# The pair loop of a graph network in the source's order on four engines, with two graphs prepared side by side

## The chip, the cores and the metric

The kernel runs on one core of a Trainium2 chip. The core's engines have queues of their own: PE (TensorE: matrix products into PSUM), DVE (VectorE: elementwise work), ACT (ScalarE: activations and copies), POOL (GpSimd: here indirect transfers and small copies) and SP (SyncE: here only the issue of DMA transfers). Each works through its instructions in the order of its queue. The metric is the time on the device in microseconds, the median of several runs.

## What is computed

The input is 16 graphs of 1024 nodes with 64 channels each, a dense 0/1 adjacency matrix of 1024 x 1024 for each graph, and a mask. Layer 0, cut to what matters:

```python
h = relu(layernorm(x))
neigh = (adj > 0) & ~eye
rank  = cumsum(neigh) - neigh                  # number of a neighbour in its row
nb    = neigh.sum(-1)
skip  = where(nb > 10, (nb + 1) // 2, 1)
rem   = neigh & (skip > 1) & (rank % skip == skip - 1) & mask
rem   = rem | rem.T
living = where(rem, 0, adj or eye) > 0
s  = sort(h of the living neighbours)          # for every node and channel
nv = living.sum()
for tau, w in ((0.25, 0.25), (0.5, 0.5), (0.75, 0.25)):
    agg += w * (s interpolated at tau * (nv - 1))
x = x + mask * (relu((h + agg) @ W1 + b1) @ W2 + b2)
```

Layer 1 is a layernorm, three graph convolutions with `adj` (each a product, a bias, a relu and a scaling), their concatenation through one more product, a relu, and the sum with `x`.

## The kernel before

Two graphs make a pair: with 64 channels each they fill the 128 partitions. There are eight pairs. For a pair the kernel first *prepares*, then *gathers* and *sorts* blocks of nodes.

**Preparing** (`prepare`, L585, with `prepare_one` for each graph of the pair, L654). Layernorm of `x` (L560 to L568) and a store of `h`. For each of eight tiles of 128 rows: a load of `adj` into tile `a` (L664, 512 KB, two buffers), its sign as `edge` on ACT (L671), a test of the values on DVE (`junk_v`, L673), eight transposes on PE (`ptE`, L678), and a copy from PSUM to `edgeT` on ACT (L681). Then a store of `edgeT` to memory (`adjT_d`, L684), sums of chunks of 128 columns, numbers of neighbours and skips (`own` L686, `nbp` L691, L695 to L706), the rank test (`cs` on PE, L716 and L721; `stays` on ACT, L725; the comparison on DVE, L726), the removal (`q` on PE, `edge` on ACT, L752), a key by which nodes are put in order of their number of neighbours (`key` L758, `keys` L763 on PE, eight passes `junk` on ACT, L770, `place` on DVE, L773), and eight indirect scatters on POOL that write the rows of the living edges by place (`live_d`, L778). Then `find_live` fetches these rows (`lp`, L794, on POOL's queue), transposes them (`pt`, L809; `liveT`, L812), and counts (`sums`, `nv_all`, `by`), and `number_slots` gives each living neighbour its slot number (`pr` on PE, L845 and L847; `r` on ACT, L851). `z` (L615 to L618) and `hp`, `h` in three parts of 16 bits (L625 to L628), come at the end.

**Gathering** (`gather`, L959). Nodes lie in order of their number of neighbours, in seven blocks (0 to 200, 392, 592, 768, 888, 960 and 1008, with 11 to 26 slots) and a tail of 16 nodes with 42 slots. For a group of slots DVE compares the slot numbers with constants (one-hot tile `s`, L987, two buffers), PE multiplies it with `hp` into `pg` (L1018, three buffers in PSUM, 48 products of up to 400 columns for a full group), and ACT copies `pg` to `g` (L1023).

**Sorting** (`quantiles`, L925, in `sort_block`). A sorting network on DVE: elementwise minima and maxima between two arrays `g` and `t` (L935). Weights of the quantiles come from two ACT passes for each slot (`coef`, L868 and L871); DVE multiplies and adds (L941, L950) into `agg`.

**The order.** `weave` (L1106) runs through the sort of block n operation by operation and calls other generators' steps by the share of the sort that is done: the gather of block n + 1 over the window −0.2 to 0.9, and the preparation of the next pair (`ahead`) in `SHARES[n]` steps of a total of 93:

```python
SHARES = (10, 9, 17, 24, 20, 13, 0)
```

Preparation goes graph after graph, copies from PSUM stand directly behind the products that they empty, and the last block of a pair runs beside block 0 of the next (L1457). This is the source's order. The queue of each engine is set by a scheduler of the framework, which takes the source's order as a priority and reorders by its own costs. A hint (`after=` in `send` and `store`, L1032 to L1053) holds back the transposes of finished aggregates. The pair loop is at L1438. Before it lies the prologue (constants, `prepare(0)`, the gather of block 0), after it the late stage (last pair, tails, MLP, layer 1).

Of the kernel before, what the change touches and what calls it, by code (L numbers as in the profile page):

```python
# [10 lines left out]
F32 = mybir.dt.float32  # L11
# [11 lines left out]
P = 128  # L23
C = 64
# [6 lines left out]
SHARES = (10, 9, 17, 24, 20, 13, 0)  # L31
# [348 lines left out]
class Steps:  # L380


    def __init__(self, gen):
        self.gen, self.result = gen, None

    def step(self):
        if self.gen is None:
            return False
        try:
            next(self.gen)  # L390
        except StopIteration as e:
            self.gen, self.result = None, e.value
            return False
        return True

    def rest(self):
        while self.step():
            pass


@with_exitstack
def graph_layers_kernel(ctx: ExitStack, tc: tile.TileContext, ins, out: bass.AP):
# [182 lines left out]
    def prepare(p, pools):  # L585
# [6 lines left out]
        xt, h, sq = room[:, 0], room[:, 1], room[:, 2].rearrange("p x t c -> p (x t) c")  # L592
        for x in range(2):
            nc.sync.dma_start(out=xt[:, x], in_=rows_of(x_d[2 * p + x]))
        flat = "p x t c -> p (x t) c"
        layernorm_relu(work, h.rearrange(flat), xt.rearrange(flat), sq, T2)
        for x in range(2):
            nc.sync.dma_start(out=rows_of(h_d[2 * p + x][:, :]), in_=h[:, x])
        yield
# [5 lines left out]
        find_live, number_slots = [], []  # L605
        for x in range(2):
            find_live.append((yield from prepare_one(st, x, pools)))
        for x in range(2):
            number_slots.append((yield from find_live[x]()))
            yield from number_slots[x](0)  # L610


        st.z = keep.tile([P, len(TAUS), N], BF16, tag="z", name="z")
        half = work.tile([P, N], F32, tag="a", bufs=2, name="half")
        nc.vector.tensor_scalar(half, st.nvs, 0.498, MAGIC, ALU.mult, ALU.add)  # L615
        nc.vector.tensor_scalar(half, half, MAGIC, None, ALU.subtract)
        for q, (tau, _) in enumerate(TAUS):
            nc.vector.scalar_tensor_tensor(st.z[:, q, :], st.nvs, -tau, half, ALU.mult, ALU.add)  # L618
# [5 lines left out]
        st.hp = keep.tile([P, 3, 2, NT, C], BF16, tag="hp", bufs=2, name="hp")  # L624
        nc.scalar.copy(st.hp[:, 0], h)  # L625
        nc.vector.tensor_tensor(h, h, st.hp[:, 0], ALU.subtract)
        nc.scalar.copy(st.hp[:, 1], h)
        nc.vector.tensor_tensor(st.hp[:, 2], h, st.hp[:, 1], ALU.subtract)  # L628
        yield
        st.number = itertools.chain(*(number_slots[x](1) for x in range(2)))  # L630
# [7 lines left out]
    def chunk_sums(eT, pools):  # L638

# [11 lines left out]
        nc.scalar.copy(sums, tot)  # L651
        return sums

    def prepare_one(st, x, pools):  # L654
        work, keep, ps = pools
# [5 lines left out]
        edgeT = work.tile([P, NT, N], F8, tag="byte", bufs=4, name="edgeT")  # L661
        def load(t):
            a = work.tile([P, N], F32, tag="a", bufs=2, name="a")
            nc.sync.dma_start(out=a, in_=adj_d[b, t * P : (t + 1) * P, :])  # L664
            return a

        coming = load(0)
        yield
        for t in range(NT):
            a, coming = coming, load(t + 1) if t + 1 < NT else None  # L670
            nc.scalar.activation(edge[:, t, :], a, AF.Sign, saturate=False)  # L671
            junk = work.tile([P, N], F8, tag="junk_v", name="junk_v")
            nc.vector.scalar_tensor_tensor(  # L673
                junk, a, 1.0, a, ALU.is_equal, ALU.not_equal, accum_out=odd[:, b, t : t + 1], saturate=False
            )
            pt = ps.tile([P, NT, P], F32, tag="big", bufs=2, name="ptE")
            for u in range(NT):
                nc.tensor.matmul(  # L678
                    out=pt[:, u, :], lhsT=edge[:, t, u * P : (u + 1) * P], rhs=ident_h, start=True, stop=True
                )  # L680
            nc.scalar.activation(edgeT[:, :, t * P : (t + 1) * P], pt, AF.Copy, saturate=False)  # L681
            yield

        nc.sync.dma_start(out=adjT_d[b][:, :, :], in_=edgeT)  # L684
        own = diagonal(edgeT)
        nc.vector.tensor_tensor(own, own, other_h[:, None, :].to_broadcast([P, NT, P]), ALU.mult, saturate=False)  # L686
        yield
        sums = chunk_sums(edgeT, pools)
# [5 lines left out]
        nb = work.tile([P, NT], F32, tag="nb", name="nb")  # L694
        nc.vector.tensor_copy(nb, nbp)  # L695


        act = work.tile([P, NT], F32, tag="act", name="act")
        nc.vector.scalar_tensor_tensor(act, nb, MIN_DEG, mk, ALU.is_gt, ALU.mult)
        skip = work.tile([P, NT], F32, tag="skip", name="skip")  # L700
        nc.vector.tensor_scalar(skip, nb, 0.5, 0.25, ALU.mult, ALU.add)
        nc.vector.tensor_scalar(skip, skip, MAGIC, MAGIC, ALU.add, ALU.subtract)
        back = work.tile([P, NT], F32, tag="back", name="back")
        nc.vector.tensor_scalar(back, skip, -3.0, 1.0, ALU.mult, ALU.add)
        look = work.tile([P, NT], F32, tag="look", name="look")
        nc.vector.scalar_tensor_tensor(look, skip, 1.0, act, ALU.add, ALU.mult)  # L706
        nc.vector.tensor_scalar(look, look, 1.0, None, ALU.subtract)
        yield
# [3 lines left out]
        for t in range(NT):  # L712
# [12 lines left out]
            nc.scalar.activation(stays[:, t, :], cs, AF.Abs, bias=back[:, t : t + 1], scale=2.0)  # L725
            nc.vector.tensor_scalar(stays[:, t, :], stays[:, t, :], look[:, t : t + 1], None, ALU.not_equal)  # L726
            if t % 2:
                yield

        nv = work.tile([P, NT], F32, tag="nv", name="nv")  # L730
        for t in range(NT):
            q = ps.tile([P, N], F32, tag="big", bufs=2, name="q")
            for hf in range(NH):
# [18 lines left out]
            nc.scalar.activation(  # L752
                edge[:, t, :], q, AF.Relu, bias=bias(-2.0), accum_out=nv[:, t : t + 1], saturate=False
            )
            yield

        key = work.tile([P, NT], F32, tag="key", name="key")
        nc.vector.scalar_tensor_tensor(key, nv, float(N), node, ALU.mult, ALU.add)  # L758
        minus = work.tile([P, NT], F32, tag="minus", name="minus")
        nc.vector.tensor_scalar(minus, key, -1.0, None, ALU.mult)  # L760
        keys = ps.tile([P, N], F32, tag="big", bufs=2, name="keys")
# [5 lines left out]
        above = work.tile([P, NT], F32, tag="above", name="above")  # L767
        for t in range(NT):
            junk = work.tile([P, N], F8, tag="junk", name="junk")
            nc.scalar.activation(  # L770
                junk, keys, AF.Sign, bias=minus[:, t : t + 1], accum_out=above[:, t : t + 1], saturate=False
            )
# [14 lines left out]
        yield  # L787
        def find_live():


            liveT = work.tile([P, NT, N], F8, tag="byte", bufs=4, name="liveT")
            def fetch(t):
                lp = work.tile([P, N // 4], I32, tag="lp", bufs=2, name="lp")
                load = nc.gpsimd.dma_start(out=lp, in_=live_d[b][t * P : (t + 1) * P, :])  # L794
# [6 lines left out]
                return lp.bitcast(F8)  # L801

            coming = fetch(0)
            yield
            for t in range(NT):
# [32 lines left out]
            def number_slots(side):  # L838

                j0, j1 = ((0, SPLIT), (SPLIT, N))[side]  # L840
                for u in range(NT):
# [10 lines left out]
                    if u % 2:  # L852
                        yield

            return number_slots

        return find_live

# [679 lines left out]
```

## Time and profile before

| what | value |
|---|---|
| runs | 3157.66, 3168.78, 3170.39 us (median 3168.78) |
| profiled execution | 3163.56 us, span 3161.8 us |
| granted clock of PE over the span | 0.915 |
| POOL's largest group: `live_d` scatters (L778) | 128, 261.1 us |
| copies of `pg` on ACT (L1023) | 384, 169.0 us busy, 399.4 us of idle time before them |

The page gives the busy time of each engine, the chain of work that ended last, and groups of instructions by line. In a group's row "<-" stands between what is written and what is read; "x" is the count; then follow the busy time and the mean in nanoseconds of one; then the engine's idle time just before instructions of this group, and what ended most of it. Idle time of an engine that isn't the bottleneck costs nothing by itself. The chain of waits gives shares of the span. In tables by window the first figures are the window and its length, then busy time of PE, PEld (weight loads), DVE, ACT and POOL with counts, then the granted clock of PE, the DMA engines' share and GB/s. Rows of waits give engine, tile and line, the releaser, the sum in us, the number of times, and the longest.

### The profile page before, as it was taken

The page shows a single profiled execution, that of the slowest core. Times are in us where ns is not written, and L with a number is a line of the kernel's source. Part 1 is how long each engine was busy: PE and PEld are TensorE (multiplying, and loading weights), DVE is VectorE, ACT ScalarE, POOL GpSimd, SP SyncE. Part 2 cuts the span into 40 slices and gives each one's busy share as a digit, 9 for nine tenths or more (in the row PEclk, how much of TensorE's full clock was granted, in tenths as well). Part 3 has the DMA queues.
Part 4 walks back from the last instruction along what each step waited for, and adds up shares of the span by engine and source line. Part 5 has one row for each costly group of instructions (what it writes and reads, how often), then busy time and mean ns, then how long its engine had stood idle before and what let it go on. Part 6 is the DMA issues. An engine that isn't in the chain of part 4 may idle for free.

```text
span 3161.8 us, 67201 instructions
## 1 busy us (share of the span) xinstructions
PE 2599.2 (82%) x27849; PEld 1697.4 (54%) x27849; DVE 2559.8 (81%) x5895; ACT 1696.2 (54%) x3292; POOL 619.5 (20%) x545
## 2 busy tenths in 40 slices
PE   2678978898888889885798889888986688977778
PEld 1445655565556556653565566456643456644445
DVE  4149889998999799989998999899976979963332
ACT  4764666567557755774367557745853223332221
POOL 5110161022102200330022103300422530311110
PEclk9779999999899999997899999999987799988989
DMA  4131022111211212122111211211113011122211
GB/s 138 46 104 60 3 67 70 56 55 52 66 57 54 64 56 68 46 72 47 42 64 51 66 56 57 67 56 63 48 36 75 9 41 26 49 55 54 54 54 42
DMA packets 221082, 177.45 MB, mean 56 GB/s; under 512 B 189024, under 2 KB 189152, under 8 KB 216672
## 3 DMA queue, kind: packets, MB, share of 16 engines
q1 hardware_dynamic: 141824, 125.88, 13.1%
q0 software_dynamic: 17408, 37.81, 3.9%
q10 hardware_dynamic: 61536, 9.39, 1.7%
q8 instruction: 219, 3.59, 0.5%
q14 instruction: 95, 0.78, 0.1%
HBM read 124.44 MB, written 48.55 MB: 55 GB/s over the span
## 4 chain that ended last, share of the span: by engine, by line
DVE 40%; PE 29%; ACT 12%; DMA 8%; issue 6%; another core or an unknown queue 2%; POOL 2%; ACTq 1%; DVEq 0%; POOLq 0%; SPq 0%
PE pg L1018 11%; DVE t L935 10%; DVE s L987 9%; DVE g L935 8%; PE pg L1200 5%; ACT junk L770 3%; DMA a<-in_adj 3%; DMA lp<-live_d 3%; DVE junk_v L673 2%; PE pr L845 2%; DVE g_tails L935 1%; DVE t_tails L935 1%; PE keys L763 1%; PE pf L1216 1%
## 5 line engine op out<-in xcount | busy, mean ns | idle before, releaser
L1018 PE MATMUL pg<-s,hp 128*64 128x400 bf16 (+11 forms) x16848 | 1366.5, 313 | 172.3 <-DVE s L987 138.1
L1018 PEld LDWEIGHTS <-hp 128*64 128x64 bf16 x16848 | 894.5, 112 | 553.9 <-issue 109.6
L987 DVE TENSOR_SCALAR s<-r 128x3200 bf16<-128x3200 bf16 (+25 forms) x1312 | 623.6, 521 | 103.6 <-PE pg L1018 74.9
L778 POOL DMA_INDIRECT live_d<-edge,place x128 | 261.1, 2040 | 1354.3 <-DVE place L773 1149.9
L1023 ACT COPY g<-pg 128x400 f32<-128x400 f32 (+10 forms) x384 | 169.0, 443 | 399.4 <-PE pg L1018 363.1
L935 DVE TENSOR_TENSOR t<-g 128x600 f32<-128x600 f32 (+9 forms) x524 | 315.5, 626 | 34.0 <-ACT g L1023 33.2
L1200 PE MATMUL pg<-adjT,xw 128*64 128x512 fp8e4 x2304 | 284.5, 398 | 52.8 <-ACT xw L1185 25.7
L935 DVE TENSOR_TENSOR g<-t 128x96 f32<-128x96 f32 (+16 forms) x555 | 283.2, 537 | 1.2
L1243 POOL DMA_INDIRECT agg<-agg_d,place x128 | 171.2, 1338 | 495.2 <-PE pt L1131 258.2
L671 ACT ACTIVATE edge<-a 128x1024 fp8e4<-128x1024 f32 x128 | 135.1, 1058 | 214.4 <-DMA a<-in_adj 213.9
L1200 PEld LDWEIGHTS <-xw 128*64 128x64 bf16 x2304 | 140.1, 114 | 182.4 <-issue 42.0
L868 ACT ACTIVATE coef<-z,bias 128x200 f32<-128x200 bf16 (+6 forms) x480 | 173.9, 405 | 102.3 <-DVE agg L950 66.0
L935 DVE TENSOR_TENSOR t<-t 128x192 f32<-128x192 f32 (+20 forms) x447 | 207.8, 475 | 0.2
L871 ACT ACTIVATE coef<-coef,wcol 128x200 f32<-128x200 f32 (+7 forms) x512 | 189.6, 403 | 9.3 <-issue 7.1
L673 DVE SCALAR_TENSOR_TENSOR junk_v<-a 128x1024 fp8e4<-128x1024 f32 x128 | 155.4, 1214 | 24.4 <-DMA a<-in_adj 24.4
L845 PE MATMUL pr<-liveT,upto 128*128 128x512 fp8e4 (+2 forms) x384 | 127.4, 350 | 53.1 <-ACT r L851 46.9
L770 ACT ACTIVATE junk<-keys,minus 128x1024 fp8e4<-128x1024 f32 x128 | 144.3, 1128 | 38.1 <-PE keys L763 34.3
L851 ACT CAST r<-pr 128x592 bf16<-128x592 f32 (+1 forms) x256 | 142.5, 585 | 41.1 <-PE pr L847 32.1
L794 POOL DMA_DIRECT2D lp<-live_d x128 | 89.4, 699 | 376.9 <-PE pt L809 319.3
L812 ACT ACTIVATE liveT<-pt 128x1024 fp8e4<-128x1024 f32 x128 | 130.3, 1034 | 50.5 <-PE pt L809 47.1
L752 ACT ACTIVATE edge<-q,bias 128x1024 fp8e4<-128x1024 f32 x128 | 141.8, 1108 | 22.6 <-PE q L747 22.6
L725 ACT ACTIVATE stays<-cs,back 128x1024 f16<-128x1024 f32 x128 | 136.7, 1111 | 31.1 <-PE cs L721 15.9
(182 smaller groups left out, 3879.4 us busy)
## 6 DMA issues: line engine op xcount, KB each, us to landing
a<-in_adj SPq DMA_DIRECT2D x128, 512.0 KB
adjT_d<-edgeT SPq DMA_DIRECT2D x16, 1024.0 KB
lp<-live_d POOLq DMA_DIRECT2D x128, 128.0 KB
adjT<-adjT_d SPq DMA_DIRECT2D x16, 1024.0 KB
room<-in_x SPq DMA_DIRECT2D x16, 256.0 KB
h_d<-room SPq DMA_DIRECT2D x16, 256.0 KB
h_again<-h_d SPq DMA_DIRECT2D x16, 256.0 KB
xt<-in_x SPq DMA_DIRECT2D x16, 256.0 KB
```

The lines of the kernel that those rows point to most:

```text
L673: nc.vector.scalar_tensor_tensor(junk, a, 1.0, a, ALU.is_equal, ALU.not_equal, accum_out=odd[:, b, t : t + 1], saturate=False)
L770: nc.scalar.activation(junk, keys, AF.Sign, bias=minus[:, t : t + 1], accum_out=above[:, t : t + 1], saturate=False)
L778: sent = nc.gpsimd.indirect_dma_start(out=live_d[b][:, :], out_offset=bass.IndirectOffsetOnAxis(ap=place[:, b, t : t + 1], axis=0), in_=ed ...
L845: nc.tensor.matmul(out=pr[:, o], lhsT=upto, rhs=liveT[:, u, sl], start=True, stop=(u == 0))
L868: nc.scalar.activation(coef[:, i, :], z[:, at], AF.Abs, bias=bias(rank - (slots + 1) // 2 + tau), scale=sign)
L871: nc.scalar.activation(coef[:, i, :], coef[:, i, :], AF.Relu, bias=wcol[:, q : q + 1], scale=-w)
L935: nc.vector.tensor_tensor(view(bufs, o, n1, n2), view(bufs, a, n1, n2), view(bufs, b, n1, n2), ALU.max if op else ALU.min)
L987: nc.vector.tensor_scalar(s[:, k, :, us, w0:], r[:, :, us, at + w0 : at + W], float(LIVE + 1 + k0 + k), None, ALU.is_equal)
L1018: summed = nc.tensor.matmul(out=pg[x * C : (x + 1) * C, ks, w0:], lhsT=st.hp[:, part, x, u, :], rhs=s[:, ks, x, u, w0:], start=(whole and ...
L1023: nc.scalar.copy(g[:, k0 : k0 + n, :], pg)
L1200: nc.tensor.matmul(out=pg[cs, :], lhsT=part[:, u, cs], rhs=adjT[x][:, u, sl], start=(u == 0 and k == 0), stop=(u == NT - 1 and k == len(xw ...
L1243: nc.gpsimd.indirect_dma_start(out=agg[:, t, x, :], out_offset=None, in_=agg_d[b][:, :], in_offset=bass.IndirectOffsetOnAxis(ap=place[:, b ...
```

## The change

The loop over pairs stands in a region in which DVE, PE, ACT and SP take their instructions in the source's order; POOL, the prologue and the late stage stay with the scheduler. The source's order is written anew:

- A step may hand back a callable (mostly the copy of a PSUM tile on ACT). `Steps` runs it at the start of the next step, so that it stands one step later in the queues. A callable may hand back another (the comparison after `stays`, the next two of the eight passes over `keys`).
- The two graphs of a pair are prepared in turns (`in_turns`), the second 22 turns behind the first. `find_live` and the first half of the numbering are part of `prepare_one`. The second half of the numbering of pair p opens the preparation of pair p + 1. Shares are new, 171 steps in all.
- Two tiles `a` are loaded ahead where one was, and two tiles `lp`. The fetch of `lp` goes from POOL's queue to SP's.
- A gather is a pipeline: step i copies group i − 2, makes the one-hot tile of group i, and multiplies group i − 1. Its window is 0 to 0.92; the tail's gather stands ahead of block 6's and ends at 0.4. The hint in `send` is gone.
- The activations of `coef` are spread over the first 0.6 of the sort.
- `z` is made by `make_z` after the last block of a pair, with the copies to `tail_z` on POOL.

The diff, cut to its core:

```diff
-SHARES = (10, 9, 17, 24, 20, 13, 0)
+SHARES = (25, 23, 30, 40, 30, 23, 0)
+
+BEHIND = 22
...
     def step(self):
+        self.left = [more for more in [f() for f in self.left] if more]
         if self.gen is None:
-            return False
+            return bool(self.left)
         try:
-            next(self.gen)
+            more = next(self.gen)
         except StopIteration as e:
             self.gen, self.result = None, e.value
-            return False
+            return bool(self.left)
+        if callable(more):
+            self.left.append(more)
         return True
...
+def in_turns(one, other, ahead=0):
+
+    results = [None, None]
+    left = [one, other]
+    while any(left):
+        for k in range(2):
+            if k and ahead > 0 and left[0]:
+                continue
+            if left[k]:
+                try:
+                    more = next(left[k])
+                except StopIteration as e:
+                    left[k], results[k] = None, e.value
+                    continue
+                yield more
+            if not k:
+                ahead -= 1
+    return results
...
-    def prepare(p, pools):
+    def prepare(p, pools, before=None):
...
+        if before is not None:
+            yield from before
...
+        sums = yield from in_turns(*(prepare_one(st, x, pools) for x in range(2)), BEHIND)
         yield
 
         h = work.tile([P, 2, NT, C], F32, tag="a", bufs=2, name="h_again")
         for x in range(2):
             nc.sync.dma_start(out=h[:, x], in_=rows_of(h_d[2 * p + x][:, :]))
...
+        yield
+        yield
+        nc.scalar.copy(hp[:, 0], h)
+        yield
+        nc.vector.tensor_tensor(h, h, hp[:, 0], ALU.subtract)
...
+        def edges(t):
+            if t < NT:
+                a = coming.pop(t)
+                nc.scalar.activation(edge[:, t, :], a, AF.Sign, saturate=False)
+                junk = work.tile([P, N], F8, tag="junk_v", name="junk_v")
+                nc.vector.scalar_tensor_tensor(
+                    junk, a, 1.0, a, ALU.is_equal, ALU.not_equal, accum_out=odd[:, b, t : t + 1], saturate=False
+                )
+                load(t + 2)
+
+        load(0)
+        load(1)
+        yield
+        yield
+        edges(0)
         yield
...
-            nc.scalar.activation(edgeT[:, :, t * P : (t + 1) * P], pt, AF.Copy, saturate=False)
+
+            def empty(t=t, pt=pt):
+                nc.scalar.activation(edgeT[:, :, t * P : (t + 1) * P], pt, AF.Copy, saturate=False)
+                edges(t + 1)
+
+            yield empty
+        yield
...
-                load = nc.gpsimd.dma_start(out=lp, in_=live_d[b][t * P : (t + 1) * P, :])
+                load = nc.sync.dma_start(out=lps[t], in_=live_d[b][t * P : (t + 1) * P, :])
...
+            share += (n1 * n2 * W + C) / total
+            while made < len(order) and made < len(order) * share / 0.6:
+                next(weights)
+                made += 1
...
+        for i in range(len(starts) + 2):
+            if i:
+                yield
+            if 2 <= i:
+                copy(starts[i - 2])
+            if i < len(starts):
+                one_hot(starts[i])
+            if 1 <= i <= len(starts):
+                sum_up(starts[i - 1])
+            if i == len(starts) // 2 + 1:
+                send(pools)
...
-        return Steps(groups()), -(-slots // per_group(block)), -0.2, 0.9
+        return Steps(groups()), -(-slots // per_group(block)) + 2, 0.0, end
...
+            st.make_z()
+            with tc.manual_schedule(engines={nc.vector.engine, nc.tensor.engine, nc.scalar.engine, nc.sync.engine}):
+                for p in range(NP - 1):
+
+
+                    ahead = Steps(prepare(p + 1, early, st.number))
...
+                        elif n == last - 1:
+                            ahead.rest()
+                            to_come = ahead.result
+                            weave(sort_block(st, n, pools), gather_block(to_come, 0, pools))
+                            to_come.make_z()
+                        elif n == last - 2:
+                            weave(
+                                sort_block(st, n, pools),
+                                gather_block(st, last, pools, (early[0], "a", 2), 0.4),
+                                gather_block(st, n + 1, pools), steps,
+                            )
...
+                Steps(st.number).rest()
```

## The prediction

> **What bounds the kernel now.** I read the page from the whole to the stage. First the engines' busy times, then the chain that ended last, then the costliest groups of instructions:
>
> ```profile
> PE 2599.2 (82%) x27849; PEld 1697.4 (54%) x27849; DVE 2559.8 (81%) x5895; ACT 1696.2 (54%) x3292; POOL 619.5 (20%) x545
> ...
> DVE 40%; PE 29%; ACT 12%; DMA 8%; issue 6%; another core or an unknown queue 2%; POOL 2%; ACTq 1%; DVEq 0%; POOLq 0%; SPq 0%
> ...
> L1018 PE MATMUL pg<-s,hp 128*64 128x400 bf16 (+11 forms) x16848 | 1366.5, 313 | 172.3 <-DVE s L987 138.1
> L987 DVE TENSOR_SCALAR s<-r 128x3200 bf16<-128x3200 bf16 (+25 forms) x1312 | 623.6, 521 | 103.6 <-PE pg L1018 74.9
> L671 ACT ACTIVATE edge<-a 128x1024 fp8e4<-128x1024 f32 x128 | 135.1, 1058 | 214.4 <-DMA a<-in_adj 213.9
> L794 POOL DMA_DIRECT2D lp<-live_d x128 | 89.4, 699 | 376.9 <-PE pt L809 319.3
> ```
>
> DVE and PE are level over the whole span, so the average decides nothing. Busy times of the prologue, the pair loop and the late stage (columns: window, PE, PEld, DVE, ACT and POOL busy, granted clock, DMA share, GB/s) do:
>
> ```profile
> 0.00:230.00 230.00, 126.68 (x1093) 81.89 (x1094) 74.52 (x226) 145.00 (x207) 67.28 (x172) 0.84 0.31 94
> 230.00:2380.00 2150.00, 1848.57 (x21340) 1211.23 (x21339) 2006.00 (x4496) 1335.58 (x2603) 380.98 (x245) 0.93 0.18 56
> 2380.00:3162.00 782.00, 623.97 (x5416) 404.26 (x5416) 479.28 (x1176) 215.60 (x484) 171.25 (x128) 0.88 0.19 46
> ```
>
> In the loop DVE works 2006.0 of 2150 us: 144 idle, 20.6 in each of seven pairs. That is all an issue order can win there. Six stretches of one pair (551 to 851 us), roughly block by block, show where it lies:
>
> ```profile
> 580.00:620.00 40.00, 33.45 (x429) 23.09 (x425) 40.00 (x57) 17.92 (x35) 0.00 (x0) 1.00 0.24 82
> 620.00:668.00 48.00, 45.77 (x565) 31.65 (x562) 48.00 (x78) 29.76 (x49) 0.00 (x0) 1.00 0.14 45
> 668.00:713.00 45.00, 39.16 (x470) 27.87 (x470) 44.07 (x86) 33.03 (x61) 22.65 (x8) 0.92 0.15 52
> 713.00:750.00 37.00, 35.11 (x396) 24.38 (x396) 36.52 (x93) 33.59 (x62) 7.37 (x10) 1.00 0.16 45
> 750.00:797.00 47.00, 38.71 (x394) 20.27 (x390) 34.67 (x135) 29.63 (x62) 12.16 (x15) 0.85 0.21 60
> 797.00:845.00 48.00, 39.71 (x412) 22.81 (x412) 42.20 (x127) 28.00 (x63) 8.66 (x3) 0.86 0.25 76
> ```
>
> Four stretches have DVE full; of the next 95 us it is idle 18.1 (47 − 34.67 and 48 − 42.20). DVE's waits within the loop say on what:
>
> ```profile
> DVE s L987 <- PE pg L1018: 70.9, 43, 10.3
> DVE t L935 <- ACT g L1023: 33.2, 7, 5.6
> DVE s L987 <- remote: 17.5, 3, 7.5
> ...
> DVE junk_v L673 <- DMA a<-in_adj: 0.9, 1, 0.9
> ```
>
> The one-hot tile waits for the gather's matmuls to release one of its two buffers. In the timeline around 750 us PE's queue stands at the second graph's transposes (`pt`): their `lp` rows come after eight scatters on POOL (748.1 to 758.7), so the matmuls behind them wait too.
>
> **What the skill says.** *TensorE: Matmul & The Clock Gate*, "Architectural detail: the array is 16× 32×32, not 1× 128×128": ScalarE and VectorE are strict FIFO, and PE may only pull weight loads forward. The trace agrees: the one-hot at 773.1 sits 7.0 us behind PE although sort operations follow in its queue. *DMA: Bandwidth & Descriptors*, "Specifications": about 1 us to the first byte from GpSimd's queue, 0.6 from SyncE's. That prices the moved `lp` load 0.4 us lower, an estimate; the trace has only the POOL form (2.4 us, issue to use). The TensorE page's "HAM oscillation — how this bites in real kernels" says that idle gaps over some 3.4 us halve the clock; here the granted clock is 1.00 in the full stretches and 0.85 in those with holes, which fits.
>
> **The change, part by part.**
>
> *Instructions.* The counts on PE, DVE and ACT don't change, and no tile changes shape. So work is moved, not removed; the saving must be idle time.
>
> *The prologue loses cover.* The scheduler had hoisted work of the next pair under the prologue's waits. The groups of 0 to 230 us have 22 `junk_v` where one pair has 16, so 6 x (1.22 + 0.08) = 7.8 us, and a second layernorm, 4 x 1.2 + 0.25 + 0.2 = 5.3. These 13.1 us of DVE move into the loop, since the ordered region begins only after block 0's gather: 2006.0 + 13.1 = 2019.1. The prologue is no shorter for it: DVE works 74.5 of its 230 us. It ended (first sort) at 230.3; ACT's queue there meets the first `liveT` copy behind the scatters, and 226 to 238 is possible. I take 233.
>
> *The late stage* stays in the scheduler's hands: 781.6 us. Outside the span lie 3163.6 − 3161.8 = 1.8 us.
>
> *Sum without loop idle:* 233 + 2019.1 + 781.6 + 1.8 = 3035.5. The profiled run (3163.6) is 5.2 us under the median (3168.8), so I add 5.2 at the end. Break-even is (3163.6 − 3035.5) / 7 = 18.3 us of DVE idle a pair, against 20.6 now. The change has to beat what the scheduler left by 2.3 us a pair only to pay for the prologue.
>
> *Loop idle that goes.* Steps are now spread by sort work (25, 23, 30, 40, 30, 23) and both graphs run side by side, so `pt` and the numbering no longer pile up in the last two blocks. Summing DVE, PE and ACT by block in the new order with this trace's mean durations gives 29.8 DVE beside 23.4 PE in the last block and 33.1 beside 28.5 in the one before. I let all 18.1 us go.
>
> *Loop idle that comes, per pair:*
> - PE in order behind DVE. The block sums (DVE/PE) are 43.1/37.6, 46.8/40.7, 50.2/50.4, 44.0/47.2, 33.5/28.1. Slack of the first two cannot be banked, since only two one-hot buffers let PE lag. Within block 0 a gather turn has 5.0 to 6.2 us of PE beside 3.5 to 4.4 of DVE (48 matmuls of 400 columns, 4.1 to 4.2 us, and a `ptE` or `cs` group), and the last step of block 3 has 17.0 beside 12.0. Walking the two sums turn by turn, DVE at most two tiles ahead, costs 4 us if every column runs at full clock and 14 at the measured durations. I take 10, as the clock was 0.93.
> - Loads of `a`. Today ACT waits for them 213.9 us and DVE 0.9, as DVE does other work. In order, `junk_v` stands in DVE's queue and everything behind it waits: sort operations, so one-hots, so PE. For the first graph tiles 0 and 1 are issued 2.15 us of DVE work before the first use and landing took 3.4 to 4.9 us here: 1.3 to 2.8 at the start, then up to 0.4 on each of eight tiles (two buffers at (4.9 + 1.5) / 2 = 3.2 us against 2.8 of DVE work a tile). Bounds 1.3 and 6; I take 4. For the second graph 4.7 us lie between, so nothing.
> - `h_again` to `hp`: load and ACT cast, 3.5 + 1.0, against 2.7 us of DVE work before the subtraction that waits in order: 2.
> - Each block's first sort operation waits for the last copy of `g`: 33.2 / 7 = 4.7 today. That gather now ends at 0.92 of the sort and the copy comes one step after the matmuls: 1 to 4; 3.
> - `key`, `compare`, `own`: each result is asked for one or two steps later. Between nothing and 4; 1.
> - Scatter to `lp`: eight scatters of 1.27 us and 2.4 landing are 12.6 us, with about 9 to 11 us of steps before `pt` in block 3 or 4. PE stands at `pt` with gather matmuls queued behind it. Bounds 1 and 5; 2. Below nothing only the queue change can go: SP takes the fetch 0.4 us earlier, and POOL's scatters of one graph no longer stand behind the other's fetches (its 319.3 us of waiting for `pt`). On SP a fetch now waits for scatters with no load of `a` behind it, since the second graph's are all out some 55 us of DVE work before.
> - `make_z` after each pair: its 4.9 us of DVE (0.69 x 2 and 3.49) are in the sum but have no cover; PE then starts the next block from one-hots already made: 0.
> - Coefficient activations spread over 0.6 of the sort: ACT works 180.7 us of some 300, hidden. If ACT's queue stands at a `liveT` copy they delay the final multiplication; that is counted in the scatter line.
>
> Together 10 + 4 + 2 + 3 + 1 + 2 = 22, bounds 7 (4 + 1.3 + 0 + 1 + 0 + 1) and 35 (14 + 6 + 2 + 4 + 4 + 5). 3035.5 + 7 x 22 = 3189.5, against the median 3195: 0.8% slower.
>
> **The rivals.**
> *A, faster.* The order is good enough that PE never falls two tiles behind, and the clock rises to 1.00 because PE has no more holes. The place is blocks 0 and 3; the price is the first item at 4 instead of 10, with `a` 1.5, `g` 2 and 1.5 for the rest: 9 us a pair, 3035.5 + 63 + 5.2 = 3104. It decides from 18.3 down. For it: the full stretches at clock 1.00. Against it: in the second stretch PE was busy 45.8 of 48 already, with less preparation in it.
> *B, no change.* The wait is exchanged at par: 18 a pair, 3035.5 + 126 + 5.2 = 3167. For it: DVE's total is the same and idle was 20.6.
> *C, much slower.* In-order PE and in-order DVE stop one another (PE at `pt` or `pr` with an ACT copy to come, DVE at the one-hot, ACT at `liveT`), holes return and the clock drops to 0.85: 33 a pair, 3035.5 + 231 + 5.2 = 3272. For it: the two stretches at 0.85. Against it: copies come a step later, which is there to prevent this.
> That the order is not what is written can't be ruled out by the source alone, but the compiled queues of the four engines follow it.
>
> **Chances.** What a measurement can tell from no change is about 0.5%, 3153 to 3185. Forecast (20.6 to 28 a pair, 3185 to 3237, its own range) 0.40, C 0.12, B 0.18, A 0.30. So slower 0.52, same 0.18, faster 0.30. The range leaves out A's lower part (under 10 us a pair; 0.13) and C's upper part (over 31; 0.07): 3108 to 3258. Faster and slower both have weight since 2.3 us a pair divides them.
>
> **What would show it.** Right: first sort at 230 to 238 us; DVE idle under 4 us in the last two blocks of a pair; `junk_v` waiting for `a` at 20 us or more where it was 0.9; the one-hot waiting for PE in blocks 0 to 3, 50 to 90 us in all; `lp` on SP's queue; late stage 782 within 5. Wrong: loop idle under 18 a pair with `a` hidden (then A), or waits of ACT for `pt` and clock under 0.9 in the loop (then C).

## The result and the profile after

The changed kernel takes 3561.05 us (median of 4 runs, 3556.72 to 3572.89), the unchanged one in the same runs 3164.51: ratio 1.126, 95% interval 1.1221 to 1.1298. That is 12.6% slower, where 0.8% was forecast. The profiled execution has a span of 3571.1 us, 409.3 over that of before.

The page first, with the lines that answer to those of before: engines, chain, groups.

```profile
PE 2653.0 (74%) x27849; PEld 1781.6 (50%) x27849; DVE 2623.7 (73%) x5895; ACT 1744.4 (49%) x3292; POOL 386.1 (11%) x417
...
PE 38%; issue 22%; DVE 19%; ACT 11%; DMA 3%; POOL 3%; another core or an unknown queue 2%; ACTq 1%; SPq 0%; DVEq 0%; POOLq 0%
...
L1096 DVE TENSOR_SCALAR s<-r 128x3200 bf16<-128x3200 bf16 (+25 forms) x1312 | 611.6, 524 | 220.5 <-PE pg L1127 210.8
...
L733 PE MATMUL ptE<-ident_h,edge 128*128 128x128 bf16 x1024 | 96.7, 250 | 231.1 <-ACT edge L717 228.5
```

The counts are the same, no engine is busy over 74%, and DVE's share of the last chain fell from 40% to 19%. Most of the time went into waiting. The table of prologue, loop and late stage, in the same columns as before:

```profile
0.00:239.40 239.40, 125.41 (x1130) 84.15 (x1131) 62.62 (x169) 129.02 (x173) 57.76 (x156) 0.86 0.25 73
239.40:2764.50 2525.10, 1907.10 (x21346) 1288.42 (x21345) 2080.45 (x4553) 1401.30 (x2640) 153.40 (x130) 0.87 0.16 49
2764.50:3571.00 806.50, 620.54 (x5377) 409.07 (x5373) 480.63 (x1176) 214.03 (x480) 174.93 (x131) 0.87 0.18 45
```

First sort at 239.4 instead of 230.3 (+9.1), loop 2525.1 instead of 2149.7 (+375.4), late stage 806.5 instead of 781.6 (+24.9). In the loop DVE is busy 74.5 us longer (2080.45 against 2006.0) and idle 444.7 instead of 143.7 us: 63.5 a pair instead of 20.6. The blocks of one pair (second of the loop) show where:

```profile
589.80:643.20 53.40, 35.92 (x366) 21.23 (x366) 44.57 (x57) 23.56 (x52) 3.02 (x3) 0.82 0.15 39
643.20:700.40 57.20, 45.47 (x523) 30.05 (x524) 47.99 (x77) 33.49 (x50) 0.00 (x0) 0.89 0.28 92
700.40:756.80 56.40, 48.79 (x616) 36.80 (x616) 51.13 (x74) 34.36 (x58) 0.00 (x0) 1.00 0.23 74
756.80:810.20 53.40, 43.38 (x530) 30.53 (x529) 45.81 (x85) 37.98 (x65) 12.07 (x8) 0.97 0.13 39
810.20:858.40 48.20, 34.38 (x350) 21.21 (x348) 34.94 (x89) 31.24 (x61) 8.76 (x8) 0.82 0.11 34
858.40:905.50 47.10, 33.30 (x367) 23.28 (x365) 34.02 (x133) 27.29 (x58) 0.00 (x0) 0.81 0.19 47
905.50:937.50 32.00, 24.89 (x298) 18.84 (x297) 31.27 (x113) 9.62 (x29) 0.00 (x0) 0.87 0.02 4
```

Before, four stretches were full and the hole was in two. Now six of seven blocks have 5 to 13 us of DVE idle each, and only the last, without preparation in it, is full. What DVE waits for in the loop:

```profile
DVE s L1096 <- PE pg L1127: 192.8, 79, 7.5
DVE key L834 <- ACT edge L826: 58.8, 14, 10.7
DVE stays L792 <- ACT stays L795: 54.1, 22, 4.5
DVE junk_v L719 <- DMA a<-in_adj: 42.8, 21, 4.3
DVE h_again L655 <- ACT hp L653: 34.3, 7, 5.9
DVE nb L763 <- PE nbp L755: 14.9, 7, 6.0
```

And what PE waits for there:

```profile
PE ptE L733 <- ACT edge L717: 182.0, 64, 19.9
PE pg L1127 <- DVE s L1096: 105.1, 33, 9.0
PE pr L942 <- ACT r L950: 61.7, 61, 13.1
PE by L919 <- ACT junk L847: 49.9, 7, 7.1
PE q L808 <- ACT edge L826: 43.5, 37, 3.3
```

In the kernel before, the rows for the numbering and the transposes read:

```profile
PE pr L845 <- ACT r L851: 45.3, 41, 7.0
...
PE ptE L678 <- ACT edgeT L681: 11.3, 26, 1.3
```

Summed by releaser over the whole answers, PE stands for ACT 57.7 us a pair, against 16.9 before, and ACT stands for PE 122.8 against 67.7. One moment in the timeline (start, length, engine, line; in brackets the idle time before it) shows how the queues hook into one another. It is the end of the first block above:

```profile
628.77 1.50 PE L1127 MATMUL pg<-s,hp 128*64 128x144 bf16 x42
...
631.77 1.22 DVE L635 SCALAR_TENSOR_TENSOR room<-room,ln_var 128x1024 f32<-128x1024 f32 x1
...
633.02 0.99 SPq L637 DMA_DIRECT2D h_d<-room  x2
...
634.88 9.10 SPq L712 DMA_DIRECT2D a<-in_adj  x4
639.48 1.06 ACT L717 ACTIVATE edge<-a 128x1024 fp8e4<-128x1024 f32 x1 [8.63 <-DMA a<-in_adj]
639.48 1.22 DVE L719 SCALAR_TENSOR_TENSOR junk_v<-a 128x1024 fp8e4<-128x1024 f32 x1 [4.28 <-DMA a<-in_adj]
640.59 1.03 PE L733 MATMUL ptE<-ident_h,edge 128*128 128x128 bf16 x8 [10.31 <-ACT edge L717]
```

On SP the loads of `a` stand behind the store of `h` (L637), which waits for the end of the layernorm on DVE (632.99); the first is issued 1.9 us after that. ACT, DVE and PE then all stand at the first tile: PE for 10.31 us, DVE for 4.28, with sort operations behind.

### The profile page after: what moved, and what is told of

It reads as the page before. It is cut to its first block, busy times and chain, and to the rows that moved or that the text cites. A ratio compares the mean times of both kernels' runs of the same rounds, so it can differ in the third digit from the quotient of the medians.

```text
span 3571.1 us, 67311 instructions
## 1 busy us (share of the span) xinstructions
PE 2653.0 (74%) x27849; PEld 1781.6 (50%) x27849; DVE 2623.7 (73%) x5895; ACT 1744.4 (49%) x3292; POOL 386.1 (11%) x417
## 4 chain that ended last, share of the span: by engine, by line
PE 38%; issue 22%; DVE 19%; ACT 11%; DMA 3%; POOL 3%; another core or an unknown queue 2%; ACTq 1%; SPq 0%; DVEq 0%; POOLq 0%
PE pg L1127 19%; PE pg L1312 4%; DVE t L1031 4%; DVE s L1096 4%; DVE g L1031 3%; ACT junk L847 3%; DMA lp<-live_d 2%; ACT edge L826 2%; PE q L808 1%; DVE g_tails L1031 1%; PE pt L895 1%; DVE t_tails L1031 1%; PE q L819 1%; PE pr L942 1%
## 5 line engine op out<-in xcount | busy, mean ns | idle before, releaser
L1127 PE MATMUL pg<-s,hp 128*64 128x400 bf16 (+11 forms) x16848 | 1406.1, 325 | 170.3 <-DVE s L1096 155.3
L1127 PEld LDWEIGHTS <-hp 128*64 128x64 bf16 x16848 | 964.1, 117 | 557.9 <-issue 167.6
L1096 DVE TENSOR_SCALAR s<-r 128x3200 bf16<-128x3200 bf16 (+25 forms) x1312 | 611.6, 524 | 220.5 <-PE pg L1127 210.8
L861 POOL DMA_INDIRECT live_d<-edge,place x128 | 150.8, 1178 | 1901.3 <-issue 1404.8
L1031 DVE TENSOR_TENSOR g<-t 128x96 f32<-128x96 f32 (+15 forms) x555 | 287.5, 542 | 4.0
L733 PE MATMUL ptE<-ident_h,edge 128*128 128x128 bf16 x1024 | 96.7, 250 | 231.1 <-ACT edge L717 228.5
L962 ACT ACTIVATE coef<-z,bias 128x200 f32<-128x200 bf16 (+6 forms) x480 | 192.6, 407 | 105.0 <-DVE agg L1053 41.1
L965 ACT ACTIVATE coef<-coef,wcol 128x200 f32<-128x200 f32 (+7 forms) x512 | 204.1, 406 | 17.3 <-issue 2.2
L733 PEld LDWEIGHTS <-edge 128*128 128x128 fp8e4 x1024 | 73.1, 112 | 255.8 <-ACT edge L717 244.8
L738 ACT ACTIVATE edgeT<-ptE 128x1024 fp8e4<-128x1024 f32 x128 | 130.8, 1025 | 104.0 <-PE ptE L733 104.0
```

The lines of the kernel that those rows point to most:

```text
L733: nc.tensor.matmul(out=pt[:, u, :], lhsT=edge[:, t, u * P : (u + 1) * P], rhs=ident_h, start=True, stop=True)
L962: nc.scalar.activation(coef[:, i, :], z[:, at], AF.Abs, bias=bias(rank - (slots + 1) // 2 + tau), scale=sign)
L965: nc.scalar.activation(coef[:, i, :], coef[:, i, :], AF.Relu, bias=wcol[:, q : q + 1], scale=-w)
L1031: nc.vector.tensor_tensor(view(bufs, o, n1, n2), view(bufs, a, n1, n2), view(bufs, b, n1, n2), ALU.max if op else ALU.min)
L1096: nc.vector.tensor_scalar(s[:, k, :, us, w0:], r[:, :, us, at + w0 : at + W], float(LIVE + 1 + k0 + k), None, ALU.is_equal)
L1127: nc.tensor.matmul(out=pg[x * C : (x + 1) * C, ks, w0:], lhsT=st.hp[:, part, x, u, :], rhs=s[:, ks, x, u, w0:], start=(whole and i == 0 an ...
```

## What was tried on the chip

Theory O: the fixed order costs the time, as each queue stands at an instruction whose input another queue has not come to. Rival S: the rewritten source costs it whatever the order. Ratios are to the unchanged kernel measured on the same chip beside the run. Its medians on the five chips were 3172.4, 3135.5 (one run), 3124.1, 3170.4 and 3169.5 us, 1.5% apart, so ratios are compared and not times. A ratio without an interval is of one run, for which 1% decides nothing. In these first diffs, `{...}` stands for the set of the four engines.

**Which order.** The first edit takes the region away:

```diff
-            with tc.manual_schedule(engines={...}):
+            with ExitStack():
```

> The changed source (new steps, shares, gather pipeline, fetch of lp on SP) without the region of fixed order: the scheduler sets all queues. Theory O (the fixed order costs the time: PE, ACT and DVE stand in front of results that the others have not made): the time comes back to about 3130 to 3230 us, DVE idle in the pair loop to 15 to 25 us a pair. Theory S (the rewritten source itself costs it: the shares, the gather window from 0, the later copies): still over 3450 us.

3201.96 us, ratio 1.0106 (1.0067 to 1.0144). The loop, in the same columns:

```profile
235.90:2389.50 2153.60, 1819.43 (x21311) 1234.62 (x21337) 2006.02 (x4496) 1333.19 (x2602) 190.83 (x133) 0.94 0.19 56
```

DVE's busy time in the loop is that of the unchanged kernel, idle is 147.6 us, 21.1 a pair. Theory O holds: this order costs about 11.5 of the 12.6%, the rewriting 1%. Then engines one at a time and in groups, by changing that set alone, such as:

```diff
-            with tc.manual_schedule(engines={...}):
+            with tc.manual_schedule(engines={nc.vector.engine}):
```

> The changed kernel with DVE alone in the source's order; PE, ACT and SP are the scheduler's. If DVE's own order is what stops everything (it asks for results of PE and ACT one or two steps after their issue), it stays at 3450 to 3600 us with the same waits (key for edge 8 us a pair, stays for stays 8). If the harm is in PE's and ACT's order, 3200 to 3300 us.

> The changed kernel with PE alone in the source's order. If PE's order does the harm (it stands at ptE for the sign of ACT 26 us a pair, with gather matmuls behind), 3400 to 3550 us and DVE's one-hot still waits over 20 us a pair for PE. If not, 3150 to 3250 us.

> The changed kernel with PE and ACT in the source's order; DVE and SP are the scheduler's. If losses add by engine (all four 397 us over the unchanged kernel, DVE alone 163, PE alone 179, each with 30 of the rewritten source): 3380 to 3430 us. If the loss is in the coupling of DVE with the others: near PE alone, 3340 to 3370 us.

> The changed kernel with ACT alone in the source's order. ACT is busy 54% of the span, so a wait in its queue has room: 3200 to 3250 us. If ACT's queue holds back the copies that PE and DVE wait for: over 3300 us, with DVE's sort waiting for g.

> The changed kernel with DVE and ACT in the source's order; PE and SP are the scheduler's. If ACT's order adds nothing to DVE's (as alone it added 15 us to the rewritten source): 3320 to 3370 us. If DVE and ACT block one another without PE: over 3420.

> The changed kernel with DVE and PE in the source's order; ACT and SP are the scheduler's. If the losses of DVE (133 over the free source) and PE (149) add: 3460 to 3500 us. If ACT's order is what makes PE's loss large (PE and ACT together lost 65 more than each by itself): 3380 to 3440. If DVE and PE share one loss: 3340 to 3380.

> The changed kernel with DVE, PE and ACT in the source's order and SP the scheduler's. If SP's order has no part: 3510 to 3570 us (1.12 to 1.13 of the unchanged kernel), with DVE's waits for loads of a as before (6 us a pair). If loads and stores in SP's fixed queue hold one another: ratio under 1.11 and the wait of junk_v for a under 2 us a pair.

| in the source's order | us | ratio | DVE idle in the second pair |
|---|---|---|---|
| none | 3201.96 | 1.011 | 17.4 |
| ACT | 3180.22 | 1.014 | 18.5 |
| DVE | 3334.91 | 1.051 | 29.2 |
| PE | 3351.36 | 1.056 | 41.5 |
| DVE, PE | 3369.26 | 1.079 | 35.7 |
| PE, ACT | 3394.65 | 1.083 | 48.4 |
| DVE, ACT | 3396.79 | 1.087 | 39.4 |
| DVE, PE, ACT | 3527.65 | 1.113 | 54.4 |
| DVE, PE, ACT, SP | 3561.05 | 1.126 | 58.0 |

DVE or PE alone is worse than I expected for a harmless one and better than for the sole culprit: neither is "the" engine. ACT alone costs 0.4%, less than one run can tell, as expected of an engine at half load; beside a fixed PE or DVE or both it costs 2.6 to 3.6%, which I had not expected with DVE. So ACT's order does harm once a neighbour's queue is fixed too; that the neighbour can't step past what ACT has not copied is my reading of it. DVE and PE together lose less than both alone would add to (1.079 against 1.097); by its time, 3369, this run fits the third case, by its ratio, about 3421 us on the first chip, the second. SP's part is about 1.3%, hardly more than one run can tell, where I had expected either none or over 1.6. With SP free `junk_v`'s wait for `a` fell from 42.8 to 9.7 us; that is 1.4 a pair, as the second theory said (under 2), while its ratio (under 1.11) was just missed:

```profile
DVE junk_v L719 <- DMA a<-in_adj: 9.7, 12, 2.2
```

Not all of the loss is waiting. The pages' first lines, for the scheduler's order and for DVE alone in the source's order:

```profile
PE 2578.3 (81%) x27819; PEld 1733.6 (54%) x27849; DVE 2559.2 (80%) x5895; ACT 1693.2 (53%) x3292; POOL 409.4 (13%) x417
PE 2583.9 (78%) x27819; PEld 1757.8 (53%) x27849; DVE 2617.1 (79%) x5895; ACT 1711.6 (51%) x3292; POOL 375.2 (11%) x417
```

With the same instructions DVE is busy 58 us longer, over two fifths of the 133 us that its order alone costs.

**Where the waits come from.** The next kernel prepares pair 0 only:

```diff
-                    ahead = Steps(prepare(p + 1, early, st.number))
+                    ahead = Steps(again(st, p))
```

> The changed kernel, four engines in order, that prepares pair 0 only: pairs 1 to 7 gather and sort the rows of pair 0 again, and the late stage reads pair 0's adjacency, places and h; so the preparation of seven pairs is left out (about 42 us of DVE work a pair, 85 to 105 of PE). Theory P (the idle time comes from preparation's handovers between PE, ACT and DVE in fixed queues; gather and sort alone run through): DVE idle under 6 us a pair, 2760 to 2830 us. Rival G (the gather pipeline itself, one-hot tile against matmuls with two buffers, stops DVE in order): idle over 20 us a pair, over 2900 us.

2914.69 us. The loop:

```profile
237.40:2121.50 1884.10, 1244.36 (x15367) 863.19 (x15366) 1819.74 (x4004) 527.16 (x1426) 18.02 (x18) 0.83 0.03 5
```

DVE's idle time is 64.4 us, 9.2 a pair, between both expectations; of it 4.4 are one-hots that wait for PE. Both expected times were wrong: my sum had left out the tails that are sorted within the loop (64 us: 1884.1 less seven pairs of 260) and the longer late stage. Gather and sort in order run nearly through; of 63.5 us, 54 come with the preparation. This kernel leaves out the preparation's work as well as its handovers; that the work alone isn't the cause shows in the first experiment, where the same work in the scheduler's order leaves 21.1 us.

**Loosening single handovers**, all four engines in order. Signs a step earlier:

```diff
         edges(0)
+        edges(1)
...
-                edges(t + 1)
+                edges(t + 2)
```

> The changed kernel, all four engines in order, but the sign of tile t + 2 instead of t + 1 is issued when tile t's transposes are emptied, so that PE's transposes find their tile signed a step before. Theory L (PE standing at ptE for ACT, 182 us in the pair loop, is the largest single loss): that wait falls under 40 us and the time by 100 to 170 us, to 3390 to 3460. Rival M (the queues are coupled everywhere; a wait taken away turns up at the next handover): the wait goes and the time falls by less than 40 us.

3532.10 us, ratio 1.113. Two of PE's waits in the loop:

```profile
PE pg L1128 <- DVE s L1097: 140.4, 44, 18.5
PE ptE L734 <- ACT edge L717: 110.0, 40, 13.2
```

72 us of the wait at `ptE` went, 35 came back where PE waits for DVE's one-hot, and 30 to 40 us of time were won (by the times and by the ratios): nearer to rival M. But 110 us of the wait stayed where theory L wanted under 40, so the edit tried that theory only in part. With this edit, 26 empty steps a pair ahead of DVE's requests:

```diff
-        yield find_skip
+        yield lambda: lambda: find_skip
+        yield
+        yield
...
-                return compare
+                return lambda: lambda: compare
...
-SHARES = (25, 23, 30, 40, 30, 23, 0)
+SHARES = (29, 27, 34, 46, 34, 27, 0)
```

> The changed kernel, four engines in order, with the sign of two tiles ahead as in the run before and 26 empty steps more for a pair, ahead of every DVE instruction that asks for a fresh result of PE or ACT: the comparison after stays 2 steps later, nb 2, key 4, the two subtractions for hp 3 each, the first junk_v 2; shares scaled to 197. Theory D (DVE stands because it asks one or two steps after the issue, while PE runs up to two one-hot tiles behind): the waits for stays, key, nb, hp (161 us in the pair loop) fall under 50 us and the time to 3380 to 3460 us. Rival M (whatever wait is removed turns up as the one-hot's wait for PE): those waits fall, the one-hot's rises, and the time stays over 3490 us.

3517.70 us, ratio 1.122. `key` waits no more (50.6 us in the run before), `stays` 33.5 (58.1) and `hp` 16.7 (33.2); but `nb` 30.4 (8.2), `junk_v` 69.1 (37.8) and the one-hot 187.2 (171.3). The sum is nearly what it was, and the time fell by 14 us while the ratio rose; theory D falls as the cause of the time, though its waits could be moved. The second graph far behind:

```diff
-BEHIND = 22
+BEHIND = 72
```

> The changed kernel, four engines in order, with the second graph 72 turns behind the first, so that the two graphs no longer hold the two preparation buffers in PSUM at the same time. Theory B (two graphs side by side leave one buffer each, so PE and ACT run in lockstep): PE's waits for ACT's copies (ptE, pr, q, by, cs) fall to half and the time by over 60 us, to under 3500 us. Rival: each graph's own chain becomes denser, each step following its own result: 3550 to 3700 us.

3852.07 us, ratio 1.229. Two of the loop's waits (the first up to 2750 us, the second up to 2900):

```profile
PE pt L895 <- DMA lp<-live_d: 225.6, 50, 23.5
DVE place L856 <- ACT junk L847: 145.0, 13, 12.7
```

A pair takes 393 us, as each step now follows directly on its own input: PE waits for the fetch of `lp` 37 us a pair over the whole loop instead of 5, and `place` for ACT's eight passes. PE's waits for ACT are 54 us a pair instead of 57.7, not half. Theory B's forecast failed, but as these new waits came with the edit, the run doesn't show what more room in PSUM would give. Of the two distances tried, 22 turns is far the better; a smaller one was not tried. The gather groups in halves:

```diff
             for i, (u, ks) in enumerate(looks):
+                if block in BLOCKS[:6] and i == len(looks) // 2:
+                    yield
```

> The changed kernel, four engines in order, with the matmuls of each gather group of blocks 0 to 5 issued in two halves, one gather step apart, so that preparation products find at most 2 us of gather ahead of them in PE's queue instead of 4.1. Theory Q (preparation's results are late because a whole group stands ahead of them): the time falls by 40 to 120 us, ratio 1.09 to 1.11, and the waits of DVE for key and stays by a third. Rival M (what is gained there is lost at the one-hot, whose buffer is released later): ratio 1.12 or more.

3520.31 us, ratio 1.110, on the border. `key` waits 51.9 (58.8), `stays` 59.7 (54.1), the one-hot 165.9 (192.8): not the waits that theory Q named. Inconclusive. Signs earlier, groups in halves, SP free and the reordered networks of the run below, together:

> The changed kernel with DVE, PE and ACT in the source's order, and together: SP free, the signs two tiles ahead, the gather groups of blocks 0 to 5 in halves, and the sorting networks' operations further apart. If the four losses are separate and add (0.011, 0.013, 0.016 and 0.003 of the unchanged time alone): ratio 1.075 to 1.09. If one coupled loss stays whatever is loosened: 1.095 to 1.115.

3486.74 us, ratio 1.1022 (1.0977 to 1.1068). The loop still has 54 us of DVE idle a pair:

```profile
237.50:2688.10 2450.60, 1900.95 (x21332) 1251.23 (x21333) 2071.94 (x4553) 1415.35 (x2639) 147.36 (x130) 0.89 0.17 50
```

PE's waits for ACT fell from 57.7 to 41.9 us a pair, DVE's idle by 9.4. This is the second case: most of the loss stays when four of its parts are loosened.

**DVE's longer busy time.** DVE alone in order, the networks' lists reordered (`hist = apart(hist)`, a list scheduling that avoids reading what was just written):

> The changed kernel with DVE alone in the source's order, as in the second run, with the operations of each sorting network reordered so that fewer read what the operation just ahead has written (30 such neighbours a pair instead of 48 by the networks' lists). Theory F (a DVE operation that reads its predecessor's output starts after its end instead of 0.08 us before it): the instructions that start after the end of the one ahead, 732 in the second run, fall by 90 to 140 and DVE's busy time by 10 to 16 us. Rival (the lost overlap has another cause): the count stays within 30.

Instructions that start after the end of the one ahead: 645 instead of 732, 87 fewer; DVE busy 2606.8 instead of 2617.1 us. The first is just under theory F's numbers, the second just within: it supports the theory. The time didn't follow: 3345.33 us, ratio 1.055 against 1.051 in the second run, within what one run can tell.

**The fetch on SP.** The unchanged kernel with `nc.sync` for `nc.gpsimd` in the fetch of `lp`:

> The unchanged kernel with one edit: the fetch of lp goes to SP's queue instead of POOL's. If the hole in the last two blocks of a pair (18 us a pair) comes from fetches and scatters that share POOL's queue, it shrinks by half and the time falls by 40 to 65 us, to 3100 to 3130. If SP's queue holds a fetch behind waits of other transfers: equal or slower, 3160 to 3220.

3206.51 us, ratio 1.0254 (1.0235 to 1.0274). DVE's largest wait is new:

```profile
DVE edgeT L686 <- DMA adjT_d<-edgeT: 107.9, 7, 16.5
```

On SP the first graph's fetch waits for its scatters, the second graph's store of `edgeT` stands behind it, and `own` waits for that store. The hole in the last block but one closed in the second pair (2.7 us instead of 12.3), and 16.8 opened two blocks earlier. With the store on ACT's queue:

```diff
-        nc.sync.dma_start(out=adjT_d[b][:, :, :], in_=edgeT)
+        nc.scalar.dma_start(out=adjT_d[b][:, :, :].bitcast(F32), in_=edgeT.bitcast(F32))
```

> The unchanged kernel with the fetch of lp on SP's queue, as in the run before, and the store of edgeT on ACT's queue instead of SP's. Theory H (on SP the fetch of the first graph, waiting for its scatters, held back the second graph's store, and DVE waited 15 us a pair for that store, while the hole in block 5 closed): that wait goes, the hole stays closed, and the time falls under the unchanged kernel's by 1.0 to 2.2%. Rival: the store waits elsewhere, or ACT's queue is held by it: ratio 1.00 to 1.03.

3160.58 us against 3170.36, ratio 0.9966 (0.9952 to 0.998): the wait is gone, the time is a little under the unchanged kernel's, and less was won than forecast, as the hole came back in part (8.3 us). It is the only version here that is faster than the unchanged kernel.

**The rewriting's 1%.** The scheduler's order, the late gathers' window as it was:

> The changed source with the scheduler's order everywhere (as the first run), and the late stage's gathers in the old window, -0.2 to 0.9, instead of 0 to 0.92. If the window costs the late stage its 24 us (each gather begins only with its neighbour's sort): late stage 780 to 790 us and ratio 1.000 to 1.006. If the longer late stage comes from the gather's pipeline of three steps: late stage over 798 us and ratio 1.008 to 1.014.

3189.10 us, ratio 1.0083 (1.0054 to 1.0111); late stage 795.0 us, after 805.8 with the new window and 781.6 in the unchanged kernel. By the traces the window is nearly half of it, between the two cases; the ratios of the two runs, 1.0106 and 1.0083, can't be told apart. The rest stays open.

## Where the prediction went wrong

*Where the difference lies.* I forecast 3189.5 us for the profiled run, which took 3572.9. Of the 383 us between, 291 are loop idle (444.7 against 7 x 22), 61 DVE's longer busy time, 25 the late stage and 6 the prologue.

*Bound and target:* right for the idle time. Of DVE's 20.6 us of idle a pair 2.3 were asked for by the prologue. Wrong was that an issue order moves idle time alone: it moves DVE's busy time too, as below.

*Readings of the trace before.* I put PE at the second graph's `pt` around 750 us. In the trace PE waits for `lp` only 2.7 us in all of 745 to 800. Of the 12.3 us of DVE idle 4.2 are a moment (752.0 to 756.3) at which DVE stands for nothing that the trace names, with ACT and for the most part PE, and 7.0 are the one-hot behind PE, which then works on the first graph's numbering (`pr`). And one of my four full stretches had a clock of 0.92, not 1.00.

*Prologue:* 239.4 us, over its bounds (226 to 238). DVE's hoisted work was 11.5 us (74.1 busy there in the first experiment, 62.6 after), not 13.1.

*"Loop idle that goes":* the last block, yes (0.7 us). The one before it kept 13.1.

*DVE's busy time, not an item of mine:* 2080.5, not 2019.1. I took busy times from a trace in which 4275 of the loop's 4495 DVE instructions start before the end of the one ahead, by 0.08 us on average. In the source's order 728 instead of 143 start 0.03 us after it, and 229 instead of 77 later still, after longer waits. Each of these 737 more loses its overlap: 737 x 0.08 = 59 us, and with the 11.5 moved 70 of the 74.5 measured; the other 4 stay open. The gaps of 0.03 us are idle time. The first experiment, with the scheduler's order, has 136 such starts.

*"Loop idle that comes", 22 us a pair, bounds 7 and 35:* this is the step that failed; measured were 63.5. By its terms, mine against the trace (sum over seven pairs divided by 7): one-hot behind PE 10 against 27.5; loads of `a` 4 against 6.1; `hp` 2 against 4.9; first sort operation on `g` 3 against none listed; "`key`, `compare`, `own`" 1 against 19.1 (58.8 + 54.1 + 5.8 + 14.9; before, `key` waited 6.9 us in the whole loop and `stays` 1.3); scatter to `lp` 2, where DVE has no wait of its own and PE stood at `pt` 5.1; and, in no item of mine, 3.6 for the 728 gaps of 0.03 us. The first and the fifth were sized far too low. Two reasons. The walk of the two sums turn by turn let PE run whenever its inputs from DVE were there. But PE stands for ACT 57.7 us a pair, which the walk left out. And I wrote "ACT works 180.7 us of some 300, hidden": true of its load and wrong of its order, as the table of engines shows, where ACT costs 0.4% alone and 2.6 to 3.6% beside another fixed queue. That PE is late, and so whatever DVE asks of PE or ACT a step or two after the issue, is my reading of these waits; no run isolates it.

*Rival C* had the kind right (queues that stop one another; loop clock 0.87, where I had 0.85; ACT waiting for `pt` 70.4 us instead of 38.8) at 33 us a pair, half of the measured. The clock is a small part: the loop's same matmuls took 1907.1 us of PE instead of 1848.6. What *TensorE: Matmul & The Clock Gate* ("HAM oscillation — how this bites in real kernels") says of idle gaps over some 3.4 us agrees in part: PE has 34 of them in the loop instead of 17, 32 end while the clock is halved, and the halved time rose from 280 to 642 us; but it lies in 80 stretches, more than there are such gaps. How much of the 58 us is clock no run isolates.

*"At SP no load of `a` behind":* right as far as it went, yet SP's fixed order still costs about 1.3%, and in the old source the same move costs 2.5%. I priced the queue by its first byte, 0.4 us, when what counts is who stands behind a waiting transfer; no run shows the 0.4.

*Late stage:* 806.5, not 782 within 5. The functions of the gather were rewritten for it too; nearly half of the difference is the window.

*What stays open:* which handover would free the rest of the coupled loss. Loosening four of its parts together won 2.4 of 12.6%. That PE and ACT in lockstep on two PSUM buffers is its core is argued from their mutual waits; a third buffer of that size was not tried. Nor was another order with other shares or a smaller distance of the two graphs, so 11.5% is the price of this order and not of every fixed one.

## What to carry to other kernels

A source order on several engines is not priced by busy sums. List for every queue what stands at its head waiting, and what is behind it; an engine at half load can become a link of the chain when its neighbours' queues are fixed too (here 0.4% alone, 2.6 to 3.6% beside another). Before moving a transfer to another queue, ask which transfer will then stand behind it while it waits. Fixing one engine's order at a time shows within a few runs whether a loss has a place or is a coupling.

## What was not expected of the hardware

Most DVE operations here start 0.08 us before the end of the one ahead; 728 in this loop start about 0.03 us after it. It seems to be those that read what the operation just ahead has written: reordering the sort so that it has fewer such neighbours took 87 away. Of the 728, 709 wait for a signal of DVE's own, but so do 765 of the 3594 that overlap, so the waits alone don't decide it. The difference is 0.11 us for each, and 585 x 0.11 = 64 us in this loop, 47 of it busy time and the rest idle. It is an estimate from these counts; no pair of operations was measured by itself.
